# Macaron layer on one core: order of the products inside a score burst, earlier LayerNorm statistics, and a new layout of the work between bursts

## The chip, the cores and the metric

The kernel runs on one core of a Trainium2 chip. The metric is the device time of one execution in microseconds; the time before is the median of three runs. Five engines work side by side, each through its own instructions in order: TensorE (PE; its weight loads are shown apart as PEld), VectorE (DVE), ScalarE (ACT), GpSimd (POOL) and SyncE (SP), which here issues nearly all DMAs.

## What is computed

Sixteen batches `b` of 512 rows and 128 columns, all fp32, go through half a feed-forward, an attention and half a feed-forward:

```python
x = x + 0.5 * ffn(layernorm(x))          # "a"
x = x + attention(layernorm(x))          # "b"
x = x + 0.5 * ffn(layernorm(x))          # "c"
# ffn(y) = y @ int4(W) + bias + (y @ A) @ B
# attention: 16 heads; queries from x, keys and values by way of a latent of 32 columns; causal softmax
```

The query and key weights are folded, so a head's score is a product over the latent's 32 columns; the value and output weights are folded too (`wvo`).

## The kernel before

**Groups and steps.** The 16 heads of a batch make 4 groups of 4 heads; a group's heads lie in the four 32-row strips of the 128 partitions. Two groups go together, and such a pair of groups takes 5 steps (`STEP`, line 524), one for each block of the causal scores. So there are 16 x 2 x 5 = 160 steps, ten for a batch (`WINDOW`). A batch's window is counted here by n mod 10, step 0 to step 9.

**A burst.** Each step has one burst of matmuls (`burst`, line 631, products recorded by `merge` at line 590). It computes two things: the scores in row form (`sx`, queries in partitions) of the current groups, of which VectorE takes the largest of each row (`find_maxima`, 600 and 604), and, six steps later (`LAG`), the same block in transposed form (`tx`, keys in partitions) with the row maxima subtracted, of which ACT takes the exponentials (`exponentials`, 613). `s_parts` (530) adds the causal mask to `sx` by short bf16 products (`eye_b,mask_w`) and the scores by long fp32 products (`kt,qt`). `t_parts` (548) makes `tx` of long fp32 products (`qt,kt`) and of short bf16 products (`rows,ones_u`) that subtract the maxima. Heads come in two pairs, with their own 64 rows of the array: pair 0 uses the first two strips, pair 1 the other two. `merge` interleaves two streams that use different strips: t of pair 0 then s of pair 0, beside s of pair 1 then t of pair 1. In before, s is always masks first, then long; t is always long first, then short.

**Buffers between engines.** `tx` tiles take four single PSUM banks in turn (tag tx), `sx` tiles two pairs of banks (tag sx). A burst's second half therefore needs banks that the work between the bursts (which takes banks with `take`, 74) has given back, and `sx` banks whose maxima VectorE has taken.

**POOL's chain.** POOL zeroes the masked blocks of the exponentials (`zeros`, 626), splits the row maxima into bf16 terms (`maxima`, 676 to 680), adds the exponentials over the keys (`add_01` 695, `add_2` 700, `add_23` 705; tiles b01 and b23), which shortens PE's row sums (`sums`, 738, products at 711), adds the bias (`with_bias`, 379), and multiplies a group's output by its reciprocal sums (`normalise`, 787). `ready_work` (907) puts the adds ahead of a burst; `normalise` stood behind the burst for both groups of a pair.

**The reciprocal sums' way.** After `sums` of a group ACT copies the sums to `ssb`, SP sends them through DRAM (`sums`, `sum`, 747 and 749), VectorE takes the reciprocal (779), and SP sends it through DRAM again so that it is spread over 32 partitions per head (`recs`, `rb`, 781 and 784). `normalise` of that group needs `rb`. It writes `ot`, which the tail's product `yp` (493) reads.

**Front and tail of a batch.** `front` (419) is a generator: loads of x (87) and of x in 32-column blocks (`z_a`, 95), statistics, 32x32 transposes on VectorE (366), the first feed-forward (`fp_a`), statistics again, the scaled rows (`ln_scale`, 355) sent through DRAM (`blocks_b`, 361, and `z_b`, 95) and transposed, then kt, queries and the latent `lat`. `tail` (483) projects the output (`yp`), adds x1, and does the second feed-forward (`fp_c`), with `blocks_c` and `z_c` on the same kind of way. Tuples of numbers (`FRONT_STEPS`, `TAIL_STEPS`, `NORMALISED_STEPS`, 479 to 481) say at which step each part is recorded: -5 for batch b is step 5 of window b - 1; a part at a whole number stands behind the burst of that step, one at .5 ahead of the next, one at .75 directly behind the next burst. The reciprocal roots of all LayerNorms of one window are taken together (`normalised`, 412): Ln and Exp on ACT (`ln_rstd`), then three Newton instructions on VectorE (`ln_newton`, 344 to 346).

The order on every engine and in SP's queue is the order of recording; nothing reorders it later.

Of the kernel before, what the change touches and what calls it, by code (L numbers as in the profile page):

```python
# [25 lines left out]
def macaron_kernel(  # L26
# [377 lines left out]
    lns = {}  # L404

    def ln_of(what, b):
        w = b + {"c": 2, "b": -1, "a": -2}[what]
        if w not in lns:
            lns[w] = ln_tile(f"w{w}")
        return lns[w]  # L410

    def normalised(w):
        whats = [k for k, b in (("c", w - 2), ("b", w + 1), ("a", w + 2)) if 0 <= b < (B - 2 if k == "c" else B)]
        ln_rstd(lns[w], whats)
        yield
        ln_newton(lns[w], whats)
        yield

    def front(b, st):


        x_sb, z = xs.pop(b), zs.pop(b)
        na, nb = f"a{b}", f"b{b}"
        la = ln_of("a", b) if b > 1 else st["first"]
        lb = ln_of("b", b) if b > 0 else st["first_b"]
        if b + 2 < B:
            xs[b + 2] = load_x(b + 2)
        if 0 < b < B - 1:
            zs[b + 1] = load_blocks(x[b + 1], f"a{b + 1}")
        ln_stats(x_sb, la, "a", (0, 1))  # L430
        yield
        ln_stats(x_sb, la, "a", (2, 3))
        yield
        xt = turn_blocks(z, na, "xt_a") if b else turn(x_sb, na, "xt_a")
        yield
        xb = with_bias(x_sb, na, nc.gpsimd if b > 1 else nc.vector)
        yield
        x1 = st["x1"] = ffn(xt, la, xb, na, "x1", 6)
        yield
        ln_stats(x1, lb, "b", (0, 1))  # L440
        yield
        ln_stats(x1, lb, "b", (2, 3))
        yield
        xn = ln_scale(x1, nb, lb)
        if b:
            z = by_way_of_dram(xn, nb)
        yield
# [5 lines left out]
        nc.vector.tensor_copy(kt, mp[:, :L])  # L453

        def query(g):
            mp = take(f"qt_ps_{b}_{g}")
            product(mp, wqk_flat[:, ts(g, P)], xnt)
            if g % 2 == 0:
                st["qt", g] = act2.tile([P, 2, L], F32, tag="qt", name=f"qt_{b}_{g}", bufs=4)
            nc.scalar.copy(st["qt", g - g % 2][:, g % 2, :], mp)  # L460

        query(0)
        yield
        query(1)
        yield
# [6 lines left out]
        query(2)  # L472
        yield
        query(3)
        yield

    FRONT_STEPS = (-19.5, -18.5, -14.5, -15, -14.25, -13.5, -12.5, -5, -3, -2.25, -1, 0.75, 3, 4)
    TAIL_STEPS = (1.75, 2.5, 2.75, 3.5, 4, 6, 6.75)  # L480
    NORMALISED_STEPS = (4, 4.5)

    def tail(b, st, late=False):

# [42 lines left out]

    T_BLOCKS = (((0, 0, 512, 0),), ((3, 384, 128, 0), (1, 128, 384, P)))

    def s_parts(sc, st, g, kind, u, pair):  # L530

        small_, large = [], []
        diag = (sc[:, :, 384:].unsqueeze(2), sc[:, :, 256:].rearrange("p k (d n) -> p k d n", d=2),
                sc.rearrange("p k (u n) -> p k u n", u=2)[:, :, :, P:])[kind]
        for s in range(NT):
            for k in range(2):
                rows = ts(2 * pair + k, LD)
                small_.append((diag[:, k, :, ts(s, LD)], mask_w[rows, s, :],
                               eye2_b[rows, : diag.shape[2], :], s == 0, False))
        for i, v, col in (((3, u, 0),), ((2, u, 0), (0, u, 384)), ((1, 0, 0), (1, 1, 256)))[kind]:  # L540
            n = (i + 1) * P
            for k in range(2):
                rows = ts(2 * pair + k, LD)
                large.append((sc[:, k, col : col + n], st["qt", g][rows, v, ts(i, P)], st["kt"][rows, :n],
                              False, True))
        return small_, large

    def t_parts(sc, st, g, kind, u, pair):

        small_, large = [], []  # L550
        for k in range(2):
            h = 2 * pair + k
            rows = ts(h, LD)
            tx = sc[k]
            if kind < 2:
                for n_, (j, q0, n, col) in enumerate(T_BLOCKS[kind]):
                    small_.append((tx[:, col : col + n], ones_u[h * LD : h * LD + 6, u, :],
                                   st["rows", g][h * LD : h * LD + 6, q0 : q0 + n], False, True))
                    large.append((tx[:, col : col + n], st["kt"][rows, ts(j, P)],
                                  st["qt", g][rows, u, q0 : q0 + n], n_ == 0, False))  # L560
            else:
                both = tx.rearrange("p (b u n) -> p u b n", b=2, u=2)
                for v in range(2):
                    small_.append((both[:, v], ones_u[h * LD : h * LD + 6, v, :],
                                   st["rows", g][h * LD : h * LD + 6, 256:].rearrange("p (b n) -> p b n", b=2),
                                   False, True))
                large.append((both, st["kt"][rows, ts(2, P)],
                              st["qt", g][rows, :, 256:].rearrange("p u (b n) -> p u b n", b=2), True, False))
        half = len(small_) // 2
        small_ = [x for two in zip(small_[:half], small_[half:]) for x in two]  # L570
        half = len(large) // 2
        return [x for two in zip(large[:half], large[half:]) for x in two], small_

    def probabilities(st, g, kind):

# [55 lines left out]
    def burst(n, s_at, t_at):  # L631
# [4 lines left out]
        for k in range(2):  # L636
            if t_at:
                tt.append([bank(f"tx_{t_at[0]['b']}_{t_at[1]}_{n}") for _ in range(2)])
                t_seq.append(sum(t_parts(tt[k], *t_at, *t_kind, k), []))
            ss.append(two_banks(f"sx_{s_at[0]['b']}_{s_at[1]}_{n}"))  # L640
            s_seq.append(sum(s_parts(ss[k], *s_at, *s_kind, 1 - k), []))
        if t_at:
            merge(t_seq[0] + s_seq[1], s_seq[0] + t_seq[1])
        else:
# [11 lines left out]
    def late_burst(t_at, i, apart=True):  # L656

        t_kind = STEP[i]
        name = f"tx_late{i}"
        tt = [[bank(name), bank(name)] if apart else two_banks(name), two_banks(name)]  # L660
        merge(*(sum(t_parts([tt[k][:, j, :] for j in range(2)] if k or not apart else tt[k], *t_at, *t_kind, k), [])
                for k in range(2)))
# [163 lines left out]

    states[0]["first"], states[0]["first_b"], states[1]["first"] = (ln_tile(k) for k in ("a0", "b0", "a1"))
# [5 lines left out]
    ln_rstd(states[0]["first"], "a")  # L835
    keep_clock(6)
    wmax_all = largest_weight(wmax)
    qscale = divide(wmax_all, seven, 1, "qs")
# [8 lines left out]
    quantised(qscale, ab)  # L847
    keep_clock(4)
    centred()
    ln_newton(states[0]["first"], "a")  # L850
    next(first)
    next(first)
    next(first)
    next(first)
    ln_rstd(states[0]["first_b"], "b")
    next(second)
    next(second)
    ln_newton(states[0]["first_b"], "b")
    ln_rstd(states[1]["first"], "a")
    keep_clock(14)  # L860
    next(first)
    next(second)
    next(second)
    next(first)
    next(first)
    ln_newton(states[1]["first"], "a")
    next(second)

    def at(n, lag=0):
# [13 lines left out]
            next(gen)  # L883
        return bool(gens)

    plan(first, 0, (0, 0.75, 3, 4))
    plan(second, 0, (0.5, 1.5))
    plan(second, WINDOW, FRONT_STEPS[7:])
    for w in range(B):
        plan(normalised(w), w * WINDOW, NORMALISED_STEPS)  # L890
    for b in range(2, B):
        plan(front(b, states[b]), b * WINDOW, FRONT_STEPS)
# [13 lines left out]

    def ready_work(n):

        for u in range(2):
            if due(n, 2 + 3 * u):  # L910
                st, g = due(n, 2 + 3 * u)
# [138 lines left out]
```

## Time and profile before

| what | value |
|---|---|
| median of 3 runs | 850.68 us (848.82 to 851.5) |
| the profiled execution | 846.34 us |
| its span, first to last instruction | 844.6 us |
| mean granted TensorE clock | 0.997 |
| chain that ended last: PE, DVE, DMA, POOL | 75%, 8%, 6%, 5% of the span |
| costliest PE group: `sx<-kt,qt` at 590 | 353.7 us, 2048 passes |
| costliest POOL group: adds at 695 | 226.7 us, 126 x 1821 ns |
| POOL idle at 676, for the maxima | 76.4 us |

How to read it: the page's first part gives each engine's busy time; the groups of its fifth part give an instruction's mean duration and who ended the idle time before it. A timeline's row has the start, the length (of all instructions of the row), the engine, the line, the output and inputs, the shape and the count. Starts of matmuls are recorded, their ends are modelled; so PE's lengths overlap, and start-to-start distances are the surer measure. A row of SP's queue shows the issue of a DMA and not its landing.

### The profile page before, as it was taken

What the parts mean: (1) busy time and instruction counts of PE and PEld (TensorE: products, weight loads), DVE (VectorE), ACT (ScalarE), POOL (GpSimd) and SP (SyncE); (2) the same over time, 40 slices, a digit from 0 to 9 for tenths busy, and PEclk for the clock granted to TensorE, in tenths of its full rate; (3) what the DMA queues carried; (4) which work ended last, traced back from release to release, by engine and by line L of the source; (5) the groups of instructions that cost most, each with busy time, mean ns of one, the idle gap of its engine ahead of it and who ended that gap; (6) DMA issues with size and microseconds to landing.
All of it is one profiled execution on the core that took longest, in us unless ns stands there. A gap on an engine that the chain in (4) does not pass through costs nothing.

```text
span 844.6 us, 35771 instructions
## 1 busy us (share of the span) xinstructions
PE 819.3 (97%) x15472; PEld 524.9 (62%) x15472; DVE 609.4 (72%) x1266; ACT 499.7 (59%) x969; POOL 679.5 (80%) x676
## 2 busy tenths in 40 slices
PE   7999999999999999999999999999999999999986
PEld 5656666665666656666565656666566665656654
DVE  7896767768686776967677686867768685766716
ACT  1156666656566655656666566666556665665651
POOL 1047898988888888988889897898879888898992
PEclk9999999999999999999999999999999999999998
DMA  5211222232132222223222231322213131221211
GB/s 121 50 28 30 54 54 67 55 67 67 42 79 67 55 66 64 65 49 79 66 55 67 60 71 45 79 66 55 67 43 67 29 75 47 55 67 32 52 31 39
DMA packets 160222, 49.10 MB, mean 58 GB/s; under 512 B 118312, under 2 KB 151880, under 8 KB 160064
## 3 DMA queue, kind: packets, MB, share of 16 engines
q1 hardware_dynamic: 159296, 46.52, 23.6%
q8 instruction: 121, 1.98, 0.9%
q10 hardware_dynamic: 768, 0.30, 0.2%
q14 instruction: 37, 0.30, 0.1%
HBM read 33.96 MB, written 12.81 MB: 55 GB/s over the span
## 4 chain that ended last, share of the span: by engine, by line
PE 75%; DVE 8%; DMA 6%; POOL 5%; SPq 2%; issue 2%; ACT 2%; DVEq 0%; POOLq 0%
PE sx L590 18%; PE tx L590 16%; PE o L711 14%; PE s L711 7%; PE yp L385 7%; PE qt_ps L385 5%; DVE nmax L600 4%; DMA z_b<-blocks_b 3%; DMA blocks_b<-xn_b 2%; POOL b L695 1%; PE fp_a L385 1%; PE kt_ps L385 1%; SPq L95 1%; POOL ot L787 1%; PE fp_c L385 1%
## 5 line engine op out<-in xcount | busy, mean ns | idle before, releaser
L613 ACT ACTIVATE pt<-tx 128x512 f32<-128x512 f32 x616 | 331.5, 595 | 104.0 <-PE tx L590 101.4
L600 DVE TENSOR_REDUCE nmax<-sx 128x2 f32<-128x768 f32 (+2 forms) x384 | 310.8, 859 | 97.2 <-PE sx L590 97.0
L590 PE MATMUL sx<-kt,qt 32*128 32x512 f32 (+3 forms) x2048 | 353.7, 454 | 0.0
L590 PE MATMUL tx<-qt,kt 32*128 32x512 f32 x1728 | 332.9, 491 | 2.8 <-DVE kt L453 2.4
L695 POOL TENSOR_TENSOR b<-pt,pt 128x768 f32<-128x768 f32 x126 | 226.7, 1821 | 2.7
L626 POOL TENSOR_SCALAR_AFFINE_SELECT pt<-pt 128x1024 f32<-128x1024 f32 (+1 forms) x162 | 145.8, 900 | 55.5 <-ACT pt L613 49.8
L590 PEld LDWEIGHTS tx<-qt,kt 32*128 32x128 f32 x1728 | 138.8, 184 | 74.9 <-issue 28.8
L590 PEld LDWEIGHTS sx<-kt,qt 32*128 32x128 f32 x2048 | 171.1, 185 | 20.9
L711 PE MATMUL o<-pt,lat 128*32 128x512 f32 x1984 | 146.4, 435 | 1.7 <-POOL pt L626 1.0
L590 PE MATMUL tx<-rows,ones_u 6*128 6x512 bf16 (+1 forms) x988 | 119.1, 294 | 0.0
L711 PEld LDWEIGHTS o<-pt,lat 128*32 128x32 f32 x1984 | 62.5, 110 | 79.6 <-issue 60.2
L604 DVE TENSOR_REDUCE nmax<-sx 128x4 f32<-128x1024 f32 x64 | 76.4, 1223 | 36.4 <-PE sx L590 36.4
L730 ACT COPY osb<-o 128x512 f32<-128x512 f32 x62 | 36.3, 586 | 89.8 <-PE o L711 89.8
L590 PE MATMUL sx<-eye_b,mask_w 32*128 32x64 bf16 (+1 forms) x2560 | 88.4, 183 | 0.4 <-DVE nmax L600 0.3
L700 POOL TENSOR_TENSOR b<-b,pt 128x512 f32<-128x512 f32 x63 | 80.0, 1270 | 5.1
L705 POOL TENSOR_TENSOR b<-pt,pt 128x512 f32<-128x512 f32 x63 | 80.4, 1275 | 0.1
L787 POOL TENSOR_TENSOR ot<-osb,rb 128x512 f32<-128x512 f32 x62 | 78.7, 1270 | 0.0
L590 PEld LDWEIGHTS <-mask_w 32*128 32x128 bf16 x2560 | 67.9, 92 | 11.8 <-issue 9.9
L460 ACT COPY qt<-qt_ps 128x512 f32<-128x512 f32 x64 | 37.2, 581 | 59.6 <-PE qt_ps L385 59.6
L590 PEld LDWEIGHTS <-ones_u 6*128 6x128 bf16 x1024 | 53.6, 93 | 27.3 <-issue 9.9
L676 POOL CAST terms<-nmax 128x32 bf16<-128x32 f32 x32 | 8.2, 255 | 76.4 <-DVE nmax L600 76.4
L385 PE MATMUL qt_ps<-xnt_b_b,wqk 128*32 128x512 f32 x512 | 66.9, 593 | 0.0
(190 smaller groups left out, 889.8 us busy)
## 6 DMA issues: line engine op xcount, KB each, us to landing
rb<-recs SPq DMA_DIRECT2D x248, 64.0 KB
x<-in_x_dram SPq DMA_DIRECT2D x16, 256.0 KB
sums<-ssb SPq DMA_DIRECT2D x248, 2.0 KB
z_a<-in_x_dram SPq DMA_DIRECT2D x60, 64.0 KB
blocks_b<-xn_b SPq DMA_DIRECT2D x15, 256.0 KB
z_b<-blocks_b SPq DMA_DIRECT2D x60, 64.0 KB
out_dram<-x_c SPq DMA_DIRECT2D x15, 256.0 KB
blocks_c<-x SPq DMA_DIRECT2D x14, 256.0 KB
```

The costliest lines, as they stand in the source:

```text
L385: nc.tensor.matmul(dst[ts(h, LD), :], lhsT=w[:, ts(h, LD)], rhs=mv, start=start, stop=stop, skip_group_check=True)
L460: nc.scalar.copy(st["qt", g - g % 2][:, g % 2, :], mp)
L590: nc.tensor.matmul(dst, lhsT=w, rhs=mv, start=first, stop=last, skip_group_check=True)
L600: nc.vector.tensor_reduce(nmax[:, i, heads, u], sx[:, :, col : col + (i + 1) * P], AX.X, ALU.max, negate=True)
L604: nc.vector.tensor_reduce(nmax[:, 1, heads, :], sx.rearrange("p k (u n) -> p k u n", u=2), AX.X, ALU.max, negate=True)
L613: nc.scalar.activation(pt[:, :, 2 * pair + k, :], tx[k].rearrange("p (b n) -> p b n", n=P), AF.Exp)
L626: nc.gpsimd.affine_select(diag, diag, pattern=[[0, diag.shape[1]], [1, P]], compare_op=ALU.is_ge, fill=0.0, base=0, channel_multiplier=-1,)
L695: nc.gpsimd.tensor_tensor(*flat, ALU.add)
L700: nc.gpsimd.tensor_tensor(b01, b01, st["pt", 2, g][:, u], ALU.add)
L705: nc.gpsimd.tensor_tensor(both, st["pt", 2, g][:, 2 + u], st["pt", 1, g + u][:, 0], ALU.add)
L711: nc.tensor.matmul(dst[ts(h, LD), :].rearrange("p (b n) -> p b n", n=P), lhsT=w[h] if isinstance(w, list) else w, rhs=mv, start=start, sto ...
L787: nc.gpsimd.tensor_tensor(turned(st)[:, g, :], st["osb", g], st["rb", g], ALU.mult)
```

## The change

1. **Order inside a burst.** `t_parts` puts the short products ahead of the long ones, but for pair 0 in the first burst of a group pair, whose `rows` have just been made. `s_parts` puts the masks behind the long products in the first stream's second part.
2. **Front.** Statistics, the first feed-forward and the loads are recorded up to a window earlier; `x` and `z_a` of the next batch are loaded together at step 9 instead of x two batches ahead, at step 0.5. `with_bias` stands ahead of the transpose. `ln_scale` with `blocks_b`/`z_b` moves from step 5 to step 7, the transpose of `z_b` from 7 to 1, kt from 7.75 (with query 0) to 6.75, `lat` behind the four queries. Batches 1 to 3 have steps of their own at the start.
3. **LayerNorm roots.** `normalised` covers b of two and a of three batches ahead (one and two before), with Ln and Exp at step 5 and Newton at step 6 (4 and 4.5 before).
4. **Tail.** The bias add and the transpose of `z_c` at step 7, `fp_c` at 7.75 (4, 6 and 6.75 before).
5. **POOL.** `normalise` of a pair's second group is recorded ahead of that step's adds, at steps 6 and 1, instead of behind the burst.
6. `x1` has 5 buffers instead of 6.

Kept as they are: every product, its shape, and all other buffers.

```diff
-        w = b + {"c": 2, "b": -1, "a": -2}[what]
+        w = b + {"c": 2, "b": -2, "a": -3}[what]
...
-        whats = [k for k, b in (("c", w - 2), ("b", w + 1), ("a", w + 2)) if 0 <= b < (B - 2 if k == "c" else B)]
+        whats = [k for k, b in (("c", w - 2), ("b", w + 2), ("a", w + 3)) if 0 <= b < (B - 2 if k == "c" else B)]
+        if not whats:
+            return
...
-        if b + 2 < B:
-            xs[b + 2] = load_x(b + 2)
         if 0 < b < B - 1:
+            xs[b + 1] = load_x(b + 1)
             zs[b + 1] = load_blocks(x[b + 1], f"a{b + 1}")
...
-        x1 = st["x1"] = ffn(xt, la, xb, na, "x1", 6)
+        x1 = st["x1"] = ffn(xt, la, xb, na, "x1", 5)
...
-    FRONT_STEPS = (-19.5, -18.5, -14.5, -15, -14.25, -13.5, -12.5, -5, -3, -2.25, -1, 0.75, 3, 4)
-    TAIL_STEPS = (1.75, 2.5, 2.75, 3.5, 4, 6, 6.75)
-    NORMALISED_STEPS = (4, 4.5)
+    FRONT_STEPS = (-31, -30.5, -28, -21, -19.25, -16, -16, -13, -9, -3.25, -2, -1, 3, 4, 5.75)
+    SECOND_STEPS = (-9.5, -8.5, -7, -4, -3.25, -2, -1, 3, 4, 5.75)
+    THIRD_STEPS = (-18.5, -18.5, -18, -17.5, -17.25, -16, -16) + FRONT_STEPS[7:]
+    FOURTH_STEPS = (-27, -26, -25) + FRONT_STEPS[3:]
+    TAIL_STEPS = (1.75, 2.5, 2.75, 3.5, 7, 7, 7.75)
+    NORMALISED_STEPS = (5, 6)
...
-    def s_parts(sc, st, g, kind, u, pair):
+    def s_parts(sc, st, g, kind, u, pair, masks_last):
...
-        return small_, large
+        return large + small_ if masks_last else small_ + large
...
-    def t_parts(sc, st, g, kind, u, pair):
+    def t_parts(sc, st, g, kind, u, pair, maxima_last=False):
...
-        return [x for two in zip(large[:half], large[half:]) for x in two], small_
+        large = [x for two in zip(large[:half], large[half:]) for x in two]
+        return small_ + large if first else large + small_
...
-                t_seq.append(sum(t_parts(tt[k], *t_at, *t_kind, k), []))
+                t_seq.append(t_parts(tt[k], *t_at, *t_kind, k, k == 0 and (n - LAG) % STEPS == 0))
...
-            s_seq.append(sum(s_parts(ss[k], *s_at, *s_kind, 1 - k), []))
+            s_seq.append(s_parts(ss[k], *s_at, *s_kind, 1 - k, t_at is not None and k == 1))
...
     def ready_work(n):
 
+        if n < N * STEPS and due(n, 10):
+            st, g = due(n, 10)
+            normalise(st, g + 1)
...
-        for u in range(2):
-            if due(n, 8 + 2 * u):
-                st, g = due(n, 8 + 2 * u)
-                normalise(st, g + u)
+        if due(n, 8):
+            normalise(*due(n, 8))
```

More of the change, by code (lines that the diff above doesn't have):

```diff
@@ L423, in front @@
         na, nb = f"a{b}", f"b{b}"
-        la = ln_of("a", b) if b > 1 else st["first"]
-        lb = ln_of("b", b) if b > 0 else st["first_b"]
-        if b + 2 < B:
-            xs[b + 2] = load_x(b + 2)
+        la = ln_of("a", b) if b > 2 else early["a", b]
+        lb = ln_of("b", b) if b > 1 else early["b", b]
         if 0 < b < B - 1:
+            xs[b + 1] = load_x(b + 1)
             zs[b + 1] = load_blocks(x[b + 1], f"a{b + 1}")
@@ L433, in front @@
         yield
-        xt = turn_blocks(z, na, "xt_a") if b else turn(x_sb, na, "xt_a")
-        yield
+        if b == 0:
+            xt = turn(x_sb, na, "xt_a")
+            yield
         xb = with_bias(x_sb, na, nc.gpsimd if b > 1 else nc.vector)
         yield
-        x1 = st["x1"] = ffn(xt, la, xb, na, "x1", 6)
+        if b:
+            xt = turn_blocks(z, na, "xt_a")
+            yield
+        x1 = st["x1"] = ffn(xt, la, xb, na, "x1", 5)
         yield
@@ L460, in query @@
             nc.scalar.copy(st["qt", g - g % 2][:, g % 2, :], mp)
+        yield
         query(0)
@@ L464, in front @@
         query(1)
+        yield
+        query(2)
+        yield
+        query(3)
         yield
@@ L471, in front @@
         yield
[L472 to L475, printed above, removed]
-    FRONT_STEPS = (-19.5, -18.5, -14.5, -15, -14.25, -13.5, -12.5, -5, -3, -2.25, -1, 0.75, 3, 4)
-    TAIL_STEPS = (1.75, 2.5, 2.75, 3.5, 4, 6, 6.75)
-    NORMALISED_STEPS = (4, 4.5)
+    FRONT_STEPS = (-31, -30.5, -28, -21, -19.25, -16, -16, -13, -9, -3.25, -2, -1, 3, 4, 5.75)
[4 more added lines that the diff above has]
+    NORMALISED_STEPS = (5, 6)
     def tail(b, st, late=False):
@@ L538, in s_parts @@
                 small_.append((diag[:, k, :, ts(s, LD)], mask_w[rows, s, :],
-                               eye2_b[rows, : diag.shape[2], :], s == 0, False))
+                               eye2_b[rows, : diag.shape[2], :], not masks_last and s == 0, masks_last))
         for i, v, col in (((3, u, 0),), ((2, u, 0), (0, u, 384)), ((1, 0, 0), (1, 1, 256)))[kind]:
@@ L544, in s_parts @@
                 large.append((sc[:, k, col : col + n], st["qt", g][rows, v, ts(i, P)], st["kt"][rows, :n],
-                              False, True))
-        return small_, large
-    def t_parts(sc, st, g, kind, u, pair):
+                              masks_last and len(large) < 2, not masks_last))
+        return large + small_ if masks_last else small_ + large
+    def t_parts(sc, st, g, kind, u, pair, maxima_last=False):
+        first = not maxima_last
         small_, large = [], []
@@ L557, in t_parts @@
                     small_.append((tx[:, col : col + n], ones_u[h * LD : h * LD + 6, u, :],
-                                   st["rows", g][h * LD : h * LD + 6, q0 : q0 + n], False, True))
+                                   st["rows", g][h * LD : h * LD + 6, q0 : q0 + n],
+                                   first and n_ == 0, maxima_last))
                     large.append((tx[:, col : col + n], st["kt"][rows, ts(j, P)],
-                                  st["qt", g][rows, u, q0 : q0 + n], n_ == 0, False))
+                                  st["qt", g][rows, u, q0 : q0 + n], maxima_last and n_ == 0, first))
             else:
@@ L565, in t_parts @@
                                    st["rows", g][h * LD : h * LD + 6, 256:].rearrange("p (b n) -> p b n", b=2),
-                                   False, True))
+                                   first and v == 0, maxima_last))
                 large.append((both, st["kt"][rows, ts(2, P)],
-                              st["qt", g][rows, :, 256:].rearrange("p u (b n) -> p u b n", b=2), True, False))
+                              st["qt", g][rows, :, 256:].rearrange("p u (b n) -> p u b n", b=2),
+                              maxima_last, first))
         half = len(small_) // 2
@@ L660, in late_burst @@
         tt = [[bank(name), bank(name)] if apart else two_banks(name), two_banks(name)]
-        merge(*(sum(t_parts([tt[k][:, j, :] for j in range(2)] if k or not apart else tt[k], *t_at, *t_kind, k), [])
+        merge(*(t_parts([tt[k][:, j, :] for j in range(2)] if k or not apart else tt[k], *t_at, *t_kind, k)
                 for k in range(2)))
@@ L825, in macaron_kernel @@
     LAG = STEPS + 1
-    states[0]["first"], states[0]["first_b"], states[1]["first"] = (ln_tile(k) for k in ("a0", "b0", "a1"))
+    early = {("a", 0): ln_tile("a0"), ("b", 0): ln_tile("b0"), ("a", 1): ln_tile("a1"), ("b", 1): ln_tile("b1")}
+    early["a", 2] = early["b", 1]
     first, second = front(0, states[0]), front(1, states[1])
@@ L834, in macaron_kernel @@
     next(first)
-    ln_rstd(states[0]["first"], "a")
+    ln_rstd(early["a", 0], "a")
     keep_clock(6)
@@ L849, in macaron_kernel @@
     centred()
-    ln_newton(states[0]["first"], "a")
+    ln_newton(early["a", 0], "a")
     next(first)
@@ L854, in macaron_kernel @@
     next(first)
-    ln_rstd(states[0]["first_b"], "b")
+    ln_rstd(early["b", 0], "b")
     next(second)
     next(second)
-    ln_newton(states[0]["first_b"], "b")
-    ln_rstd(states[1]["first"], "a")
+    ln_newton(early["b", 0], "b")
+    ln_rstd(early["a", 1], "a")
     keep_clock(14)
@@ L865, in macaron_kernel @@
     next(first)
-    ln_newton(states[1]["first"], "a")
+    next(first)
+    ln_newton(early["a", 1], "a")
     next(second)
@@ L884, in parts, with second_normalised @@
         return bool(gens)
-    plan(first, 0, (0, 0.75, 3, 4))
-    plan(second, 0, (0.5, 1.5))
-    plan(second, WINDOW, FRONT_STEPS[7:])
+    def second_normalised():
+        ln_rstd(early["b", 1], "ba")
+        yield
+        ln_newton(early["b", 1], "ba")
+        yield
+    plan(first, 0, (0, 3, 4, 5.75))
+    plan(second, WINDOW, SECOND_STEPS)
+    plan(second_normalised(), 0, (1.75, 2))
     for w in range(B):
@@ L891, in macaron_kernel @@
     for b in range(2, B):
-        plan(front(b, states[b]), b * WINDOW, FRONT_STEPS)
+        plan(front(b, states[b]), b * WINDOW, {2: THIRD_STEPS, 3: FOURTH_STEPS}.get(b, FRONT_STEPS))
     for b in range(B - 2):
```

## The prediction

> **What bounds the kernel now.** I read the page's busy rows first, then TensorE's (PE's) waits, then timelines of single bursts, then the queues behind them.
>
> ```profile
> PE 819.3 (97%) x15472; PEld 524.9 (62%) x15472; DVE 609.4 (72%) x1266; ACT 499.7 (59%) x969; POOL 679.5 (80%) x676
> ```
>
> PE is the bound: a shorter PE program shortens the run, and a wait put in front of PE lengthens it. The page's clock row is 9 in all slices but the last, so the clock is not the subject. I call step 0 to 9 the ten bursts of one batch's window; two windows take 99.09 us (the products kt_ps start at 403.20 and again at 502.29), 49.54 each. "Busy" hides what happens inside a burst, so here is the burst of a step 0, by start and modelled length:
>
> ```profile
> 435.89 0.70 PE L590 MATMUL tx<-qt,kt 32*128 32x512 f32 x2
> 435.90 0.26 PE L590 MATMUL sx<-eye_b,mask_w 32*128 32x32 bf16 x8
> 436.02 0.67 PE L590 MATMUL sx<-kt,qt 32*128 32x512 f32 x2
> 436.42 0.59 PE L590 MATMUL tx<-qt,kt 32*128 32x512 f32 x2
> ```
>
> Each fp32 product appears as two passes. A pass in full flow takes 0.43 us (436.53 to 436.96 in the same row group) and is listed with 0.59. The first tx pass is listed with 0.70 and its second pass starts 0.53 later: about 0.10 of weight load is bare, since nothing ran in those rows before it. The first sx pass behind the short mask products is listed with 0.67: 0.08 is bare, since a 25 ns mask cannot cover the next load.
>
> Second, stalls in a burst's middle. Of the step 1 and step 6 bursts, which do the same products, the one from 414.98 to 417.29 takes 2.31, that from 439.65 to 442.69 takes 3.04. The reason stands in VectorE's timeline just before:
>
> ```profile
> 436.24 0.49 DVE L344 SCALAR_TENSOR_TENSOR e_w<-mv_w,y_w 128x12 f32<-128x12 f32 x1 [1.99 <-ACT y_w L339]
> 436.76 1.20 DVE L345 SCALAR_TENSOR_TENSOR e_w<-e_w,y_w 128x12 f32<-128x12 f32 x1
> 438.00 1.20 DVE L346 SCALAR_TENSOR_TENSOR r_w<-e_w,y_w 128x12 f32<-128x12 f32 x1
> 439.13 2.34 DVE L600 TENSOR_REDUCE nmax<-sx 128x2 f32<-128x1024 f32 x2
> ```
>
> The LayerNorm's Newton steps sit ahead of the maxima of step 5, whose first half was complete at about 437.1. The maxima free the sx banks, so the next burst's masks start only at 440.39. Third, the wait for z_b on its way through DRAM:
>
> ```profile
> PE kt_ps L385 <- DVE rec L779: 4.1, 6, 0.9
> PE tx L590 <- DVE kt L453: 2.4, 7, 0.4
> ```
>
> (The releaser named rec stands behind the late transpose of z_b; VectorE waited 12.3 us in 7 times for that DMA.)
>
> **The change, part by part.**
>
> *Burst order.* In the first stream (t of pair 0, then s of pair 0) the row now is short t, long t, long s, masks. A bare bf16 load costs some 0.02; a short t of 256 columns or more lasts at least 0.107, as long as an fp32 load. So the first stream loses 0.10 + 0.08 - 0.02 = 0.16. The second stream (masks, long s, t) keeps its bare 0.08. The burst ends with the later stream: above, s's last pass starts at 437.69 and ends at 438.12, while the second stream's short t starts at 437.82 and ends at 438.03. So about 0.08 comes off, not 0.16. The other kinds give 0.08 too by the same subtraction; in steps 2, 4, 7 and 9, part of it from a long t whose load queued behind masks (listed 0.56 for 0.49 at 431.70). Where the maxima's rows are fresh the old order stays in pair 0, and 0.08 is still won. 154 bursts x 0.08 = **-12.3 us**. [...] The 0.70 and 0.67 rows show loads bare at the head of a stream and behind masks; I take the rows.
>
> *Newton and rstd* go from behind step 4 to behind steps 6 and 5. Newton now follows the maxima of step 6, after which VectorE is free until step 7's first half, some 2.6 us later; even at the slow 2.9 us it delays maxima that are not needed for another 2 us. The 14 stalls of 3.04 - 2.32 = 0.72: **-10.1 us**.
>
> *z_b and kt.* The scaled rows leave at step 7 and are turned at step 1, about 17 us later instead of 10, and kt moves to step 6.75. The kt waits (step 8 bursts such as 499.08 to 502.29 = 3.21 against 2.345, six times, 4.6 us in all) and the six half-burst waits for kt's copy (3.00 against 2.335: 4.0 us) go: **-8.6 us**. Together -31.0.
>
> *Odd groups' normalise* on POOL now comes ahead of the odd adds instead of behind them. Nothing is added, but POOL works in order: if rb has not landed, the adds wait, and behind the adds the sums on PE, and behind those the next burst. *The loads*: x and z_a go out at step 9 and blocks_b/z_b at step 7, so on SP's in-order queue stand, from the end of group 3's sums: sums, sum, blocks_b, z_b, recs and rb of group 2, out, x, z_a, recs and rb of group 3. The trace has nearly this chain, in a stretch where it is harmless:
>
> ```profile
> 426.07 1.13 SPq L747 DMA_DIRECT2D sums<-ssb  x4
> 428.25 0.34 SPq L749 DMA_DIRECT2D sum<-sums  x1
> 428.69 0.38 SPq L781 DMA_DIRECT2D recs<-rec  x1
> 430.19 1.71 SPq L784 DMA_DIRECT2D rb<-recs  x4
> 431.94 0.43 SPq L361 DMA_DIRECT2D blocks_c<-x  x1
> 434.32 1.98 SPq L95 DMA_DIRECT2D z_c<-blocks_c  x4
> 436.71 0.34 SPq L781 DMA_DIRECT2D recs<-rec  x1
> 438.66 1.71 SPq L784 DMA_DIRECT2D rb<-recs  x4
> ```
>
> The sums on PE ended at 425.32; the last rb's data ends at 441.6 (DMA share by windows: 0.43 before, 0.02 after). That is 16.3 us. The new chain has besides it out 0.45, x 0.45, z_a 2.44 (issue to next issue elsewhere in the queue's timeline), and the first recs now stands behind z loads too (1.95 to its rb instead of 1.50): +0.45. Sum 20.0. [...] By issue alone 20.0, by the rule 21.5; I take 20.8.
>
> When is it needed? After group 3's sums PE does burst 8 (2.27), fp_c 0.90, a query 0.97, burst 9 (2.26) = 6.4. From the end of burst 9 to group 1's sums the trace has 408.06 to 424.12 = 16.06; fp_a for lat adds 0.48, three bursts take off 0.24, and the product that needs b01 starts 0.22 in: 16.5. Together 22.9. POOL's work between:
>
> ```profile
> 415.44 3.59 POOL L695 TENSOR_TENSOR b<-pt,pt 128x768 f32<-128x768 f32 x2
> 419.11 1.28 POOL L700 TENSOR_TENSOR b<-b,pt 128x512 f32<-128x512 f32 x1
> 420.34 0.63 POOL L626 TENSOR_SCALAR_AFFINE_SELECT pt<-pt 128x512 f32<-128x512 f32 x1
> 420.94 1.27 POOL L787 TENSOR_TENSOR ot<-osb,rb 128x512 f32<-128x512 f32 x1
> ```
>
> normalise 1.2 and the adds 4.95 (415.44 to 420.39) are 6.15. So rb must land 16.7 after the sums; it lands at 20.8, and PE waits **4.1 us** (3.3 to 4.8), first part of it perhaps in yp, which needs the same normalise. It happens where x and z_a are loaded ahead and a batch is being normalised: 10 windows, **+41 us** (33 to 48). Four later windows without loads: 0.3 each, +1.2. The mirror case, group 1's rb at step 6, is not lengthened and comes out even: rb lands 9.0 after burst 4, adds end 15.1, needed at 15.15; I take 0 (up to 0.4 x 14 = 6).
>
> *The rest at nothing, with its cover.* The bias adds (1.28 each) go to steps 2 and 7, where POOL waits for exponentials anyway (1.47 before the 423.68 mask); uncovered, 1.28 per window. Statistics of x, the transposes and lat change steps on VectorE, behind maxima with over 2 us to the next half burst. Queries in another order, x1 in 5 buffers (it lives 42 of 50 steps): nothing. *Start*: fp_a of batch 2 falls into clock-keeping time (-1) and the z_b wait goes (-1), but VectorE gets a Newton, a transpose, four scalings and batch 2's statistics before the maxima of steps 3 to 5: about +3.5. Net +1.5 (-1 to +3).
>
> **Sum** against the profiled execution (846.34; span 844.6): -31.0 + 41 + 1.2 + 1.5 = +12.7, so 859.0. It lies 4.34 under the median 850.68; on the median's scale **863 us**.
>
> **Rivals.** *The loads land in time (other side).* One mechanism: recs and rb of group 3 overlap the loads ahead of them. At a landing up to 16.7 after the sums nothing waits: 850.7 - 28.3 = 822; at 18.2 it is 837. Even is at 19.6 (2.83 a window). For it: the chain here is made of medians, and POOL has no such wait in before. Against it: 16.3 is already used up without out, x and z_a. 830 as its middle. [...] *POOL becomes the bound by load*: 85.9 busy of 99.1 in the window 403.2 to 502.3, so 43 of the 47.3 that PE would need; not by itself: 850.7 - 28.3 + up to 6 = 828.
>
> **Numbers.** Wait at the sums of 3.3 to 4.8: 0.58 (855 to 870). Order worthless or further stalls: 0.10 (870 to 880). A wait near even, 2.5 to 3.1: 0.08, about 847 to 853. In time: 0.24 (822 to 840). A measurement here tells 0.3% (2.6 us) from no change: faster 0.24, same 0.08, slower 0.68. The range goes into the in-time case to 834 and up to 876; the likeliest case alone is 855 to 870.
>
> **What would show it.** Right: POOL's ot L787 waits for DMA rb<-recs in total some 40 us or more, PE's s L711 waits for POOL b some 30 to 40; step 6 bursts of 2.24; first tx pass at 0.59; no wait for z_b. Wrong: rb landing under 17 us after the sums; bursts still at 2.32 (order); bursts of 3 us (Newton).

## The result, and the profile after

929.84 us, median of 4 runs (924.38 to 931.83), against 850.65 in the runs beside it: 1.092 times before, 95% interval 1.087 to 1.098. The direction was as forecast, the size was not: +79 us instead of +12.7. The profiled execution took 924.38 us (span 922.6; before 846.34 and 844.6), so it is 78 us to explain.

From the page of the kernel after: busy rows, the clock row, and the chain that ended last.

```profile
PE 827.8 (90%) x15464; PEld 525.0 (57%) x15464; DVE 619.9 (67%) x1269; ACT 490.2 (53%) x971; POOL 677.3 (73%) x676
...
PEclk6899989999899999999999999998999998999998
...
PE 39%; POOL 22%; DMA 16%; SPq 9%; DVE 7%; issue 3%; ACT 3%; POOLq 0%; DVEq 0%; ACTq 0%
```

PE was 97% busy and had 75% of the chain; now it has 39%, and POOL, DMA and SP's queue have 47%. PE is not the bound any more. The clock row has 8s in its middle, where before had a 9 in every slice but the last.

The three largest waits of PE (in all, times, longest), and the largest of POOL:

```profile
PE s L725 <- POOL b L714: 53.7, 23, 3.4
PE yp L385 <- POOL ot L801: 10.8, 9, 2.7
PE o L725 <- POOL pt L639: 8.3, 10, 2.1
```

```profile
POOL ot L801 <- DMA rb<-recs: 119.3, 36, 6.9
```

The place is the one forecast (ot waits for rb, s waits for b), but there are 23 waits of s and not 10: 14 at group 1's sums (40.7 us), as forecast, and 9 at group 3's (13.0 us), the mirror case that the prediction took as 0. A third kind, of o, is new. No wait for z_b is left. One window, first on SP's queue from the end of group 3's sums on PE at 439.35:

```profile
440.09 1.10 SPq L761 DMA_DIRECT2D sums<-ssb  x4
...
444.89 1.92 SPq L95 DMA_DIRECT2D z_b<-blocks_b  x4
446.86 0.49 SPq L795 DMA_DIRECT2D recs<-rec  x1
449.95 1.71 SPq L798 DMA_DIRECT2D rb<-recs  x4
...
452.80 2.16 SPq L95 DMA_DIRECT2D z_a<-in_x_dram  x4
455.06 0.43 SPq L795 DMA_DIRECT2D recs<-rec  x1
458.43 1.71 SPq L798 DMA_DIRECT2D rb<-recs  x4
```

then on POOL:

```profile
462.08 1.26 POOL L801 TENSOR_TENSOR ot<-osb,rb 128x512 f32<-128x512 f32 x1 [5.62 <-DMA rb<-recs]
463.30 3.58 POOL L709 TENSOR_TENSOR b<-pt,pt 128x768 f32<-128x768 f32 x2
466.96 1.26 POOL L714 TENSOR_TENSOR b<-b,pt 128x512 f32<-128x512 f32 x1
```

Both waits from recs to rb take over 3 us where the prediction's chain had 1.95 (and 0.8 in all for data in the queue). rb is there 22.7 us after the sums (20.8 forecast) and POOL has been idle for 5.6. On PE two waits come of it, in yp and in group 1's sums:

```profile
463.40 1.30 PE L385 MATMUL yp<-wvo,ot 128*32 128x128 f32 x40 [1.46 <-POOL ot L801]
468.27 1.31 PE L725 MATMUL s<-b,ones_f 128*32 128x384 f32 x16 [3.35 <-POOL b L714]
```

The sums end at 469.5, 4.8 us later than without these two. PE by stretches: length, busy time and products, granted clock, then the DMA engines' share and GB/s:

```profile
464.50:469.40 4.90, 1.54 (x32) 0.96 0.00 0
469.40:473.10 3.70, 3.70 (x52) 0.60 0.02 7
```

After the wait PE runs at part of its clock: the burst of step 3 takes 3.63 us instead of 2.25. In slices of 0.6 us the clock is 0.50 from 469.0 to 472.0, after PE had been idle from 465.0 to 468.3. After an idle stretch of the same length later on (736.7 to 740.1) it stays at 1.00. Elsewhere in this trace the clock also fell to 0.50 behind shorter waits, of 2.1 us (290.6) and 2.4 us (301.3), and stayed at 1.00 behind one of 2.8 us (869.4). So here the length of a wait does not tell by itself whether the clock falls.

The burst of step 6, by start and modelled length, answers to the 0.70 row of before:

```profile
481.28 0.39 PE L603 MATMUL tx<-rows,ones_u 6*128 6x512 bf16 x2
481.51 0.59 PE L603 MATMUL tx<-qt,kt 32*128 32x512 f32 x2
```

The first long tx pass is listed with 0.59 where it had 0.70. Bursts are 2.23 to 2.26 us for 2.32 to 2.35, and the burst of 3.04 is 2.23. So the gains of the sum are in the trace, and lie under the waits.

**The waits form a loop.** Marking the end of each group's sums on PE (the start of the next product) and the start of its normalise on POOL, a window splits into four legs (means of the ten windows that begin at group 3's sums of batches 1 to 10, the last of them without loads, us):

| kernel | sums 3 to normalise 3 | to sums 1 | to normalise 1 | to sums 3 | window |
|---|---|---|---|---|---|
| after | 22.3 | 7.7 | 17.7 | 7.5 | 55.3 |
| loads_zb | 15.0 | 9.5 | 18.7 | 7.5 | 50.7 |
| zb_late | 17.6 | 7.8 | 18.5 | 7.4 | 51.4 |
| clock_fill | 22.4 | 7.2 | 19.2 | 7.5 | 56.2 |
| after_old_order | 23.0 | 7.5 | 18.3 | 7.3 | 56.1 |
| shift_32 | 22.6 | 7.6 | 18.3 | 7.3 | 55.8 |
| shift_192 | 22.8 | 7.6 | 18.8 | 7.4 | 56.6 |

The four legs add up to the window in any kernel; that a leg is a wait shows in the second and fourth. There 7.2 is POOL's normalise and adds (6.2) and the last products of the sums (1.0): where it stands, PE was waiting for POOL, and POOL began when rb came. It is 8.1 in windows of after where these last products ran at a clock of 0.50, and 9.5 in loads_zb, where group 1's sums do not wait. Group 3's sums lead through DRAM and POOL to group 1's sums, these through DRAM and POOL to the next group 3's. No burst of PE lies on that way, only the last products of the sums. PE's own work in a window, without waits, is 47.7 us (kernel best below).

### The profile page after: what moved, and what is told of

The parts are those of the page before. It is cut to its first block, busy times and chain, and to the rows that moved or that the text cites. A ratio compares the mean times of both kernels' runs of the same rounds, so it can differ in the third digit from the quotient of the medians.

```text
span 922.6 us, 35698 instructions
## 1 busy us (share of the span) xinstructions
PE 827.8 (90%) x15464; PEld 525.0 (57%) x15464; DVE 619.9 (67%) x1269; ACT 490.2 (53%) x971; POOL 677.3 (73%) x676
## 4 chain that ended last, share of the span: by engine, by line
PE 39%; POOL 22%; DMA 16%; SPq 9%; DVE 7%; issue 3%; ACT 3%; POOLq 0%; DVEq 0%; ACTq 0%
POOL b L709 11%; PE sx L603 9%; PE tx L603 7%; DMA rb<-recs 7%; DMA recs<-rec 7%; PE o L725 6%; PE s L725 5%; SPq L798 5%; DVE nmax L613 4%; POOL ot L801 4%; POOL b L714 4%; PE qt_ps L385 4%; SPq L95 3%; PE yp L385 2%; DMA blocks_c<-x 2%
## 5 line engine op out<-in xcount | busy, mean ns | idle before, releaser
L613 DVE TENSOR_REDUCE nmax<-sx 128x2 f32<-128x768 f32 (+2 forms) x384 | 315.7, 864 | 199.8 <-PE tx L603 158.9
L626 ACT ACTIVATE pt<-tx 128x512 f32<-128x512 f32 x616 | 320.6, 598 | 99.3 <-PE tx L603 94.7
L603 PE MATMUL sx<-kt,qt 32*128 32x512 f32 (+3 forms) x2048 | 337.8, 458 | 0.0
L603 PEld LDWEIGHTS sx<-kt,qt 32*128 32x128 f32 x2048 | 185.3, 194 | 26.5 <-issue 5.5
L639 POOL TENSOR_SCALAR_AFFINE_SELECT pt<-pt 128x1024 f32<-128x1024 f32 (+1 forms) x162 | 144.6, 900 | 19.4 <-ACT pt L626 16.7
L603 PEld LDWEIGHTS tx<-qt,kt 32*128 32x128 f32 x1728 | 136.4, 191 | 6.6
L725 PE MATMUL s<-b,ones_f 128*32 128x384 f32 x992 | 72.3, 413 | 53.7 <-POOL b L714 53.7
L603 PE MATMUL tx<-rows,ones_u 6*128 6x512 bf16 (+1 forms) x988 | 114.1, 307 | 1.6 <-DVE wvo L292 0.5
L758 ACT COPY ssb<-s 128x512 f32<-128x512 f32 x62 | 36.3, 586 | 123.7 <-PE s L725 121.7
L603 PEld LDWEIGHTS <-ones_u 6*128 6x128 bf16 x1024 | 44.1, 94 | 85.6 <-issue 72.3
L725 PEld LDWEIGHTS s<-b,ones_f 128*32 128x32 f32 x992 | 30.3, 116 | 87.9 <-POOL b L714 60.2
```

What stands on the lines that cost most here:

```text
L603: nc.tensor.matmul(dst, lhsT=w, rhs=mv, start=first, stop=last, skip_group_check=True)
L613: nc.vector.tensor_reduce(nmax[:, i, heads, u], sx[:, :, col : col + (i + 1) * P], AX.X, ALU.max, negate=True)
L626: nc.scalar.activation(pt[:, :, 2 * pair + k, :], tx[k].rearrange("p (b n) -> p b n", n=P), AF.Exp)
L639: nc.gpsimd.affine_select(diag, diag, pattern=[[0, diag.shape[1]], [1, P]], compare_op=ALU.is_ge, fill=0.0, base=0, channel_multiplier=-1,)
L725: nc.tensor.matmul(dst[ts(h, LD), :].rearrange("p (b n) -> p b n", n=P), lhsT=w[h] if isinstance(w, list) else w, rhs=mv, start=start, sto ...
```

## The experiments

The theory after this first look: *the late rb and POOL's order together* make the waits. Rival A: normalise ahead of the adds is costly in itself. Rival B: clock or chip. Rival C: the loads of x and z_a alone. The medians of before beside the runs were 851.4 to 851.8.

**norm_back** (in after)

```diff
-        if n < N * STEPS and due(n, 10):
-            st, g = due(n, 10)
-            normalise(st, g + 1)
...
-        if due(n, 8):
-            normalise(*due(n, 8))
+        for u in range(2):
+            if due(n, 8 + 2 * u):
+                st, g = due(n, 8 + 2 * u)
+                normalise(st, g + u)
```

> After, with the normalise of both second groups behind the burst again. My theory (rb of group 3 lands about 22.7 us after its sums, and POOL hands this wait on through the adds to PE's sums): the waits of PE's s for POOL b go from 53.7 us to under 5; what stays is about 2 us of yp in ten windows, because rb is as late as before, and the late pt ahead of o (8 us): 850 us (842 to 860). Rival A (the place of normalise alone is at fault, rb is not late for anyone else): 825 or less. Rival B (the clock or the chip's state, not the wait): above 900.

Measured 856.5 us, 1.005 (1.003 to 1.008). No wait of s for b is left; yp waits 17.8 us for ot and o 8.3 for pt, as the theory has it (one wait of s, 1.0 us at the very end, is in before too). Rival A's 825 and rival B's 900 fall.

**before_norm** (in before: the reverse of that diff)

> Before, with the normalise of the second groups put ahead of the adds, nothing else. My theory: in before rb of group 3 lands some 12.7 us after its sums, before POOL comes to it; so nothing waits in step 1, and at most about 0.5 us in step 6: 851 us (848 to 858). Rival A (the place alone is at fault): 880 to 925.

Measured 855.0 us, 1.0035 (1.001 to 1.006). In before, with windows of 49.5 us, the place costs 3 us. But s waits for b 12.8 us at group 3's sums of nine windows here, more than I had allowed: POOL's order needs a spare time that rb of group 1 does not have even in before.

**loads_early**

```diff
-        if 0 < b < B - 1:
+        if 0 < b < 4:
...
+    for b in range(4, B - 1):
+        plan(loaded(b), b * WINDOW, (LOAD_STEP,))
```

`loaded` holds the two loads, LOAD_STEP is -34, and z_a has three buffers.

> After, with x and z_a loaded three steps sooner (behind step 6, where SP's queue is empty), with a third z_a buffer; normalise stays ahead of the adds. My theory: rb of group 3 then lands some 20 us after its sums, as in the last windows of after that have no loads; waits of 2 to 3.5 us at the sums stay in most windows, the clock drops go: 875 us (865 to 888). Rival C (x and z_a are the whole cause): 825 to 835.

Measured 902.1 us, 1.057 (1.050 to 1.064): neither. Rival C falls. My own figure was too low because it counted only the waits of step 2 (27.9 us in this profile, of a run of 914.2 us); those at group 3's sums are nearly as large here (25.8).

**loads_zb** (the same, and)

```diff
-    FRONT_STEPS = (-31, -30.5, -28, -21, -19.25, -16, -16, -13, -9, -3.25, -2, -1, 3, 4, 5.75)
+    FRONT_STEPS = (-31, -30.5, -28, -21, -19.25, -16, -16, -9.5, -7, -3.25, -2, -1, 3, 4, 5.75)
```

> The same, and blocks_b and z_b issued behind rb of group 3 instead of ahead of recs of group 2 (the transpose of z_b two steps later). My theory: SP's chain ahead of rb of group 3 is short, rb lands some 13 to 15 us after the sums, no wait at the sums, clock near 1.0; up to 1 us a window may stay at group 3's sums (rb of group 1): 828 us (822 to 840). Rival A (the place of normalise alone): above 880.

Measured 870.4 us, 1.022 (1.017 to 1.027), not 828. The leg of group 3 shrank to 15.0 us and the wait at group 1's sums is gone (one of 1.0 us is left at the very end), as expected. What is left stands at group 3's sums, 1.1 to 4.5 us in each of 14 windows, because POOL waits for rb of group 1:

```profile
PE s L726 <- POOL b L715: 34.3, 15, 4.5
```

That is the mirror case, which the prediction took as even.

**best** (loads_zb and norm_back together)

> After with the loads at step 6, blocks_b and z_b behind rb of group 3, and the normalise of both second groups behind the burst again. If the two late rb (group 3's and group 1's) behind POOL's order are all that took the gains, no s, yp or o waits, the clock is near 1.0 and the three gains of the sum stay: 828 us (822 to 836). If something else in the new front (statistics, transposes, the queries' order) costs too: above 840.

Measured 826.5 us, 0.970 (0.968 to 0.972): faster than both kernels. Its page:

```profile
PE 796.4 (97%) x15464; PEld 513.9 (62%) x15464; DVE 601.0 (73%) x1269; ACT 490.1 (59%) x971; POOL 677.8 (82%) x676
...
PE 79%; POOL 6%; ACT 6%; DVE 5%; issue 2%; DMA 1%; SPq 1%; DVEq 0%; POOLq 0%; ACTq 0%
```

PE is the bound again; ten windows of 47.73 us are alike to 0.02 us. The rest of the change brings most of what the sum said: 25 us of 29.5.

best, norm_back, loads_zb and after are all four combinations of the two halves of the cost. From best's 826.5, the new SP queue alone (norm_back, 856.5) costs 30.0 us, the place of normalise alone (loads_zb, 870.4) 43.9, both (after, 929.8) 103.3. Each costs by itself, and both together 29 more than the sum of the two.

**zb_late** (after with the diff of FRONT_STEPS alone)

> After with only blocks_b and z_b issued behind rb of group 3; x and z_a stay at step 9, normalise stays ahead of the adds. Closed chain: group 3's way to rb loses some 5 us of z_b and keeps 3 us of loads, about 17 us; loop 17 + 7.2 + 18 + 7.2 = 49.4 against 47.7 of PE, 14 windows: 853 us (845 to 865). If the loads are what makes rb late: above 890.

Measured 878.3 us, 1.031 (1.025 to 1.037), above both ends of the forecast. z_b ahead of recs is worth more than the loads (902 with the loads moved). The leg came to 17.6, near the 17 expected, the other to 18.5, and both POOL legs (7.8 and 7.4) are near 7.2: the loop is closed in most windows, at 51.4 us and not 49.4.

**clock_fill** (in `sums`, group 1 only)

```diff
+        if u == 1 and g == 0:
+            for _ in range(8):
+                nc.tensor.matmul(s_ps[:, :P], lhsT=ident, rhs=ident, start=True, stop=True, skip_group_check=True)
         sum_products(st, g, u, s_ps)
```

> After, with eight idle 128x128 fp32 products (some 2.2 us) ahead of group 1's sums, that is inside the wait of step 2; the wait itself is not shortened. If the slow step 3 bursts (3.6 to 4.3 us for 2.25) come from the clock that falls to 0.50 after an idle stretch over some 3 us: these bursts come back to 2.25 and about 1.7 us x 10 go, of which up to 10 us may come back at group 3's sums, which lose that slack: 917 us (910 to 925). If they are slow for another reason (ports, DMA): 930, bursts unchanged.

Measured 944.9 us, 1.109 (1.106 to 1.113): both wrong. The bursts of step 3 are 2.25 us in all windows (3.63 at the low clock in the window of after above), so idling did lower the clock; but the time grew. On a loop without PE a faster burst only makes the next wait longer: group 3's sums now wait in every window, and the low clock turns up in step 8 of several windows (bursts of 3.4 to 3.9). That explains why nothing was gained; the 15 us that were lost stand in the DRAM leg behind group 1's sums, 19.2 for 17.7. So the clock looks like a symptom, but the fill changed more than the clock (see shift_32 and shift_192).

**loads_act** (in after: x and z_a issued by ACT)

```diff
-            xs[b + 1] = load_x(b + 1)
+            xs[b + 1] = load_x(b + 1, nc.scalar if b > 3 else nc.sync)
... (load_blocks likewise)
```

> After with x and z_a of batches 5 and later issued on ACT's queue at the same step instead of SP's. Closed chain, if only the issue time on SP (2.9 us) goes and the data still stands ahead of recs: group 3's way 20 us, as with loads_early: 897 us. If the other queue's data no longer stands ahead of recs and rb (1.7 us more): 870. No effect (930) if SP's order is not what delays rb.

Measured 946.5 us, 1.110 (1.105 to 1.114): none of the three. The leg did shrink to 19.8, but ACT was held up by its own issues (row by start and length):

```profile
233.83 5.69 ACTq L95 DMA_DIRECT2D z_a<-in_x_dram  x4
239.57 0.60 ACT L626 ACTIVATE pt<-tx 128x512 f32<-128x512 f32 x1 [6.25 <-DMA z_a<-in_x_dram]
```

The exponentials behind them came 5 to 6 us late, and the burst of step 0 took 5.8 to 8.0 us in the ten windows with loads. Whether data in another queue stands ahead of recs this run does not tell.

**before_order** (in before: `s_parts`, `t_parts` and the calls of after)

> Before with the new order inside the bursts alone. By the rows shown (bare weight loads of 0.10 and 0.08 us): bursts of 2.24 for 2.32, 154 x 0.08 = -12 us, 839 us (836 to 842). [...]

Measured 851.1 us, 0.999 (0.998 to 1.001). The bursts are 2.24 us, as the rows had it, yet the time is the same. PE's waits tell where it went (4.1 us in 6 times before):

```profile
PE kt_ps L385 <- DVE rec L784: 10.8, 9, 2.0
```

The wait for z_b, which hit every second window, now hits nearly every one, and the Newton stall grew from 0.72 to 1.0.

**best_old_order** (best with the bursts of before)

> The fastest version so far (loads at step 6, z_b behind rb of group 3, normalise behind the burst) with the old order inside the bursts. There PE has no wait left, so by both theories the order is worth 154 x 0.08 = 12 us here: 839 us (836 to 842). If a bare load were no cost: 826.

Measured 836.4 us, 0.982 (0.979 to 0.985), against 0.970 for best: the order is worth 9.9 us where PE is the bound.

**after_old_order** (after with the bursts of before)

> After with the order inside the bursts as before, all else kept. New theory (closed chain): the window of after is set by a loop in which PE's bursts have no part: group 3's sums, DRAM, normalise and adds on POOL, group 1's sums, DRAM, normalise and adds, group 3's sums of the next batch, 22 + 7.5 + 18 + 7.3 = 55 us. Then slower bursts only shorten PE's waits: 930 us (924 to 935). If waits add to PE's time, as the prediction's sum has it: bursts of 2.32 instead of 2.24 cost 12 us, 942.

Measured 941.2 us, 1.104 (1.099 to 1.108), against 1.092 (1.087 to 1.098): 11 us more, as if waits added to PE's time, and against my loop. But the table shows the extra 0.8 us of a window in the two DRAM legs, in which no burst lies. What could tie these to PE's program?

**shift_32, shift_192.** The trace lists the packets of every DMA queue. Queue 8 has 121 packets of 16 KB, one for each 256 of PE's instructions (15,464 products and as many weight loads): by this count PE's own program. In after, 28 of the 62 waits from recs to rb had such a packet starting within 1.1 us ahead of the issue of recs to 1.8 us behind it (limits chosen on this trace), and lasted 2.70 us on average; the other 34 lasted 1.79, the longest 2.31. Two recs of group 0, with nothing else under way, from issue to rb's issue: first clock_fill, 3.27 us,

```profile
q1 hardware_dynamic: 288, 0.02, 5.7%
q8 instruction: 1, 0.02, 2.5%
```

then after, 1.56 us:

```profile
q1 hardware_dynamic: 288, 0.02, 11.4%
```

The same 288 packets, with and without one instruction packet. To test it, a few tiny products at the start move all later packets against the work:

```diff
     keep_clock(14)
+    idle = bank("idle")
+    for _ in range(16):
+        nc.tensor.matmul(idle[:LD, :LD], lhsT=ident_b[:, :LD], rhs=ident_b[:, :LD], start=True, stop=True)
```

shift_192 has 124 of them and no `keep_clock(14)`, which is 56 instructions.

> After with 32 more PE instructions (16 tiny bf16 products) in the idle stretch at the start, so that each later 16 KB packet of PE's instructions comes 32 instructions sooner against the work. If these packets delay recs, z_b and z_c: counted on the trace of after, 30 to 33 of the 91 such waits would be hit instead of 23, each worth some 1 us, less what the loop hides: 937 us (931 to 945). If they don't matter: 930 (926 to 933).

> The same with 192 more PE instructions in the same place: 19 to 22 hits by the same count, 926 us (918 to 932); if the packets don't matter 930 (926 to 933). The count is rough, since a hit moves all later ones; a difference of 5 us or more between the two shifted kernels, in either direction, speaks for the packets.

Measured 928.3 (921.5 to 932.8) and 939.8 us (939.2 to 940.6); 1.089 (1.085 to 1.093) and 1.104 (1.102 to 1.107). The third window starts 2.5 and 4.0 us later than in after; without that it is 925.8 and 935.8. My count had the sign wrong and shift_32 by itself shows nothing, but the two differ by 11.5 us, over the 5 set beforehand, and by 10 without the start. In the new traces 31 and 42 waits of recs, z_b and z_c are hit by the rule above (after 32, and not the 23 of the forecast, which another count gave; after_old_order 31, clock_fill 37), and the recs that are hit take 2.76 and 2.82 us for 1.81 and 1.84. Eleven hits more, at some 1.0 us each, fit the 10 us, though after itself, with 32, lies 4 us above shift_32. So differences of 10 us between kernels on this loop can come without a burst in it. For after_old_order the number of hits does not explain the difference, only where they fall could; that stays open.

**before_order_newton** (before_order with NORMALISED_STEPS = (4, 4.75))

> The same, and the Newton steps behind the maxima of step 5 instead of ahead of them (a half step later). My theory: the 14 bursts of 3.04 us in step 6 become 2.24, another -10 us: 829 us (825 to 834). If the stall has another cause or goes to the next maxima: 837 or more.

Measured 875.0 us, 1.026 (1.024 to 1.028). Not the Newton term: at 4.75 Newton (2.9 us) and a transpose (0.7) stand between the maxima of step 5 and those of step 6, and the burst of step 6 takes 4.65 us. So the term was tested from the other side:

**best_newton_early** (best with NORMALISED_STEPS = (4.5, 4.5))

> The fastest version (loads at step 6, z_b behind rb of group 3, normalise behind the burst) with the roots and Newton ahead of the burst of step 5 again, as in before. Newton term of the prediction: step 6 bursts of about 3.0 for 2.23, 14 x 0.72 = 10 us: 836 us (833 to 840). If the place of Newton was not what stalled these bursts: 826.

Measured 846.5 us, 0.995 (0.994 to 0.997), 20 us over best and not 10. VectorE's timeline:

```profile
341.49 1.00 DVE L344 SCALAR_TENSOR_TENSOR e_w<-mv_w,y_w 128x12 f32<-128x12 f32 x1 [1.54 <-ACT y_w L339]
342.53 1.21 DVE L345 SCALAR_TENSOR_TENSOR e_w<-e_w,y_w 128x12 f32<-128x12 f32 x1
...
343.86 2.35 DVE L614 TENSOR_REDUCE nmax<-sx 128x2 f32<-128x1024 f32 x2
```

The maxima again stand behind Newton, whose first two instructions took 1.00 and 1.21 us and the third 0.17, and the burst of step 6 takes 3.38 us for 2.23. A window is 1.03 us longer (14.4 us in 14 windows); the first full window begins 4.9 us later.

## Why the prediction was wrong

*Burst order, -12.3.* Right in mechanism, near in size: 9.9 us between best and best_old_order. The loads listed as bare did cost time: with the order alone changed (before_order) the bursts fell from 2.32 to 2.24 us. What the sum missed is that a gain on PE counts only where no other wait takes it up: 0 in before_order.

*Newton, -10.1.* Right. Undoing it costs 20 us in best: 1.03 a window, and 5 us at the start. That is not quite the stall of before (0.72), since the roots stood half a step later in this test; 20 and the 9.9 of the order are already more than the 25 that all gains made.

*z_b and kt, -8.6.* No such wait is left in after or best. Not tested alone. All gains with the start came to -25 us in best (851.5 to 826.5); the sum had -29.5.

*The start, +1.5.* The 18th step's burst ends at 107.5 us, in before at 106.4: right.

*The cost, +41 and +1.2.* Place and mechanism were right: ot waits for rb, adds and sums behind it. At the place that was forecast the size was near, too: 10.8 us in yp and 40.7 at group 1's sums. The whole was not, for three reasons:

1. **The mirror case, "I take 0 (up to 0.4 x 14 = 6)".** This is the step that failed. With everything else as in best, the place of normalise alone costs 43.9 us (loads_zb), and the wait stands at group 3's sums, for rb of group 1. The prediction had it even by 0.05 us (15.1 against 15.15), from one stretch of before, where the last rb is issued 13.3 us after group 1's sums (425.32 to 438.66). In before's own windows that way alternates between 13.0 to 13.4 and 14.4 to 15.5 us; the stretch was one of the short ones. In after rb of group 1 came 10.4 us after burst 4 in the window shown (9.0 forecast), and the leg is 17.7 on average where the same stretch gave 16.3.
2. **The landing.** 22.4 us instead of 20.8 (20.0 by issue) in the ten windows with loads: the two waits from recs to rb took 2.4 and 2.6 instead of 1.95 each, and 3.9 instead of 2.9 passed from the issue of the last rb to the normalise. The 0.8 us in the 20.8 that stood for data in the queue (half the way from 20.0 to 21.5) is shown by no run; what the runs showed in its place is these longer waits, over all 62 of after 2.70 us on average with a packet of queue 8 beside them and 1.79 without. Of the four windows without loads, set at 17.0 and 0.3 us of wait, three had 20.0 to 21.2, and their sums waited 1.8 to 3.4; in the fourth rb came by 14.5 and nothing waited.
3. **The form of the sum.** 4.1 us were added to PE's window as the only wait. With the forecast's own legs the loop gives the same: 20.8 + 7.2 + 16.3 + 7.2 = 51.5, against 47.3 + 4.1 = 51.4. But with both waits live nothing takes up an excess, and all four go into the window: 22.3 + 7.7 + 17.7 + 7.5 = 55.3 by the means, 7.6 over PE's 47.7. From group 3's sums of batch 0 to those of batch 14 after takes 765.3 us and best 664.8: 100 us, where the sum had 42. With the gains of 25 that is +75, near the 78 measured.

*The clock, "not the subject".* It fell to 0.50 behind the waits, in 11 windows, for 3.4 us at a time or 6.8. Of the 100 us just named, PE's products take 32 (691.7 us busy for 659.6, by the modelled ends) and its idle time 68. On the loop only the last products of the sums feel it, 0.5 us a window. clock_fill gained nothing by keeping the bursts of step 3 fast, which speaks against the clock as the cause but is no clean test. That the term could stay at nothing was luck: the prediction gave no reason why a wait of 4 us should leave the clock alone.

*The rivals.* "In time" was wrong: but for the last window no rb of group 3 landed by 16.7. "POOL the bound by load" was wrong: at 82% busy in best it delays next to nothing.

## What to carry to other kernels

When an in-order engine is made to wait for a round trip, draw the way on from there until it comes back to its own start: if every leg is a wait, the period is the sum of the legs, and a faster former bound need not help (clock_fill gained nothing; after_old_order's 11 us stay open). Where a wait is held to be even, look at its spread over all windows and not at one stretch: here 13.3 us stood for a way that takes 13.0 to 15.5. Operations whose input is late belong behind those that others wait for, and short round trips ahead of long loads in a queue; here both together turned 1.09 times into 0.97.

## What was not expected of the hardware

PE's own program, by the count above, is a DMA customer. In after 16 KB for each 256 instructions came every 7.1 us on queue 8 (median; the middle half at 6.4 to 8.1), and a recs that met such a packet took 2.7 us instead of 1.8. PE itself shows no cost of them: best's windows are alike to 0.02 us with some seven packets in each. Moving the packets changed the time by 10 us (shift_32 to shift_192, without the start).
